# A state-space and MLP layer on one core: a third product with C on GpSimd, the fronts of images 2 and 3 raised in rank, and each norm's squares as one instruction

## The chip, the cores and the metric

The kernel runs on one core of a Trainium2 chip. The metric is the device time of the program in microseconds, as the median of its runs: 3404.53 us before the change (three runs, 3401.29 to 3411.84). The profiled execution has a span of 3393.6 us. The engines are named as the profile names them: PE is TensorE (matmuls), PEld its weight loads, DVE is VectorE, ACT is ScalarE, POOL is GpSimd, SP issues nearly all transfers.

## What is computed

The input is x of 8 images with 384 channels and 32 x 32 places (1024 tokens each), all in float32. One layer is applied:

```python
x = x + conv(_ln_c(x), ...)          # a selective state space, then an MLP
t = _to_tokens(x)
t = t + ffn(_ln_t(t), W1, b1, W2, b2)
```

The state-space part normalises each token, projects 384 channels to 2 x 768 (xm and z), runs a causal convolution of three taps and silu over xm (xc), projects xc to a step size dt, and to B and C of 16 states each, and then goes over the 1024 tokens of each image with

```python
hst = dA_t * hst + dBu_t                       # 768 x 16 states
y   = jnp.einsum('bdn,bn->bd', hst, C_t)       # sum over the 16 states
```

with dA = exp(dt A) and dBu = dt xc B. Then y + xc D is multiplied by silu(z), projected back to 384 channels (out_proj), and sent through an MLP 384 - 1536 - 384 with an exact gelu. The ffn that follows works with sign-binarised weights and quantises its activations over whole images by their largest absolute value. By its grouping of the batch it changes only images 0 to 4 (`NUM_GROUPS` is 5, one image each); images 5 to 7 get nothing from it.

## The kernel before, in words

**Stages.** For each image b there are four. The front `s1` (L523) loads x in two halves of 512 tokens, normalises (`norm`, L466), does the first projection (p_in) with the taps on DVE (L590), then xc, dbc, dt, dt x xc on POOL (L639), and the gate z (p_z). It hands dt, dt x xc, xc, z and the rows of B and C on through DRAM. The scan `s2` (L655, `scan` L668) does the recurrence. The back `s3` (L824) does out_proj (p_out) and the MLP (p_h, p_o). The `ffn` (L1022) follows for images 0 to 4 (p_y). Once, after the scan of image 0 is written down, `binarise` (L902) prepares the ffn's weights on PE, ACT and POOL.

**The scan.** It goes unit by unit, 12 in an image. A unit has four quads q of states, and each quad two tiles i = 0, 1: eight tiles of 128 x 1024. `scan_tile` (L782) takes for each tile these steps: exp on ACT writes da into PSUM (two buffers); POOL multiplies dtx with B into u (L798; u has nine buffers in SBUF); the recurrence runs on DVE (L802); then the product with C. That product is made on DVE (L819: the scan is written over da in PSUM, the product into u), or on POOL (L816: the scan is written over u, and POOL multiplies u in place). `on_pool` (L778) decides: before, tiles with i = 1 and odd q. Image 0 and image 7 are scanned in two halves of 512 tokens, and then a tile's two channel groups each have an own exp and scan of 512 columns, and the last state is kept (L810 on POOL, L813 on ACT). After each two quads (BATCH) TensorE sums the four tiles' states into py (`sums`, L719 to 732), which frees their u. At the end of a unit DVE adds xc D (L759) and POOL multiplies with z (L769).

**The order of the work.** The kernel first writes down all operations with a cost in microseconds, what they read and write and which buffers they take (`Plan.add`, L172). `Plan.run` (L216) then walks through a planned time and emits for each engine in turn the operation to do next, so that each engine has one fixed order, known before the run. `rank` (L250) sorts the operations that are ready: lane -1 (the sums) and lane 0 (the scan) first, then the fronts (lanes 1, 4, 11, 14) of images up to the one after that being scanned, then the rest, and fronts of later images last. On DVE and POOL operations that are not of the scan are preferred (L244). SLACK (L79) is a lag that the plan adds before the sums may start. Where TensorE would idle for over 0.7 us in the plan and an mm buffer is free, it emits fillers (`fill`, L375: a matmul of 256 columns on ones whose result nobody reads)[...].

**The norm.** `norm` sums over channels with three matmuls on ones (L473), subtracts the mean on DVE (L478), squares each of the three 128-channel blocks on ACT as an own instruction into one of two sq buffers, and after each square does four small matmuls on ones for the variance (L491 to 499). Then come sqrt on ACT, a reciprocal on DVE (L505), four matmuls that spread it (L512), and a multiplication on DVE (L517). The kernel has 26 norms.

```python
first = (1, b) if b <= scanned + 1 else (3, b)               # L259, the fronts
return POOL_TILES and i == 1 and q % 2 == 1                  # L780, on_pool
```

Of the kernel before, what the change touches and what calls it, by code (L numbers as in the profile page):

```python
# [26 lines left out]
F32 = mybir.dt.float32  # L27
AF = mybir.ActivationFunctionType
# [5 lines left out]
P = 128  # L34
B, C, L = 8, 384, 1024
KC = C // P
# [7 lines left out]
T = 512  # L44
# [8 lines left out]
TG = T // G  # L53
POOL_TILES = True
# [20 lines left out]
SIGNAL = 0.1  # L75
IDLE = 0.7
EARLY = 2
PATIENCE = 0.0
SLACK = 1.6  # L79
LOAD_TABLE = 1.29  # L80


def c_act(n):
    return 0.22 + n * 0.00084
# [10 lines left out]
class Clock:  # L95
# [4 lines left out]
    def __init__(self):  # L100
        self.window, self.busy, self.slow = 0, 0.0, True
# [38 lines left out]
class Fixed:  # L140


    ring = None
# [15 lines left out]
class Plan:  # L159
# [56 lines left out]
    def run(self):  # L216
# [6 lines left out]
        left, scanned = len(self.ops), 0  # L223
# [26 lines left out]
        def rank(op):  # L250


            lane, b = op.prio[:2]
            if lane <= 0:
                first = (lane, b)
            elif lane == 7:
                first = (EARLY, b)
            elif lane in (1, 4, 11, 14):
                first = (1, b) if b <= scanned + 1 else (3, b)  # L259
            else:  # L260
                first = (2, b)
            return (*first, op.prio[2])

        while left:
# [10 lines left out]
            if op.prio[0] == 0:  # L275
                scanned = max(scanned, op.prio[1])
            left -= 1
            if e == "PE":
                while now - free[e] > IDLE and self.spare.ring.free[0:] and (
# [3 lines left out]
                    ring = self.spare.ring  # L283
# [35 lines left out]
class Layer:  # L319
    def __init__(self, ctx, tc, a, out):  # L320
        self.tc, self.nc, self.a, self.out = tc, tc.nc, a, out
        self.plan = Plan()

        def pool(name, **kw):
            return ctx.enter_context(tc.tile_pool(name=name, bufs=1, **kw))

        self.const = pool("const")
        sbuf, psum, dram = pool("sbuf"), pool("psum", space=PSUM), pool("dram", space=DRAM)

        def ring(tag, bufs, where=sbuf):  # L330
            def make(shape, name):
                return where.tile(shape, F32, tag=tag, name=name, bufs=bufs)

            return Ring(make, bufs)

        self.rings = {

            "front": ring("front", 2), "t_f": ring("t_f", 2), "w_f": ring("w_f", 3),
            "dbc": ring("dbc", 1), "halo": ring("halo", 2),

            "dt_r": ring("dt_r", 3), "dtx_r": ring("dtx_r", 3), "u": ring("u", 9),
            "xr": ring("xr", 1), "zr": ring("zr", 1), "state": ring("state", 1),
            **{f"bc{i}": ring(f"bc{i}", 1) for i in range(2 * NQUAD)},
            "da": ring("da", 2, psum), "y": ring("y", 1, psum),

            "yg": ring("yg", 1), "hid": ring("hid", 2), "t_b": ring("t_b", 1), "w_b": ring("w_b", 3),
            "w6": ring("w6", 2), "w6_n": ring("w6_n", 2), "res": ring("res", 2),

            "t_n": ring("t_n", 2), "small": ring("small", 12),

            "mm": ring("mm", 3, psum), "sq": ring("sq", 2),
            "rstd": ring("rstd", 2),
        }

        def handed(name, shape):
            return Fixed(dram.tile(shape, F32, name=name))

        self.dram = {}
        for b in range(B):
            for name in ("dt", "dtx"):  # L360
                self.dram[name, b] = handed(f"{name}_d{b}", [DI, L])

            for name in ("xc", "z", "yg"):
                self.dram[name, b] = handed(f"{name}_d{b}", [NP, P, T])
            self.dram["rows", b] = handed(f"rows_d{b}", [2 * NS, L])
            if b < NQ:
                self.dram["mid", b] = handed(f"mid_d{b}", [C, L])
                self.dram["y1", b] = handed(f"y1_d{b}", [P, KH, L])
        self.bin = {
            "W1": handed("bin_w1", [KH, P, KC, P]), "W2": handed("bin_w2", [KC, P, KH, P]),  # L370
        }
        self.constants()

        self.plan.spare = self.piece("mm", [P, T], "spare")
        self.plan.fill = lambda: self.nc.tensor.matmul(  # L375
            self.plan.spare.real[:, : 2 * P], self.ones,
            self.ones.unsqueeze(1).to_broadcast([P, 2, P]), start=True, stop=True,
        )

    def piece(self, ring, shape, name):  # L380
# [3 lines left out]

    def constants(self):
        nc, a, const = self.nc, self.a, self.const
        self.ones = const.tile([P, P], F32, name="ones")
        nc.vector.memset(self.ones, 1.0)
        self.ident = ident = const.tile([P, P], F32, name="ident")
        make_identity(nc, ident)  # L390

        self.fold = const.tile([P, DQ], F32, name="fold")
        nc.vector.tensor_reduce(
            self.fold, ident.rearrange("p (d n) -> p d n", n=SQ), AX.X, ALU.add
        )
        self.edge = const.tile([P, KD, 2], F32, name="edge")
        self.eps_m = const.tile([P, 1], F32, name="eps_m")
        nc.vector.memset(self.eps_m, E1 * E2)
        self.eps_f = const.tile([P, 1], F32, name="eps_f")
        nc.vector.memset(self.eps_f, E_FFN)  # L400

        def vec(name, k):
            v = const.tile([P, k], F32, name=f"v_{name}")
            nc.scalar.dma_start(v, a[name])
            return v

        self.ln_w, self.ln_b, self.mlp_b2 = vec("ln_w", KC), vec("ln_b", KC), vec("mlp_b2", KC)
        self.conv_b, self.dt_b = vec("conv_b", KD), vec("dt_proj_b", KD)
        self.d_pair, self.d_unit = vec("D_pair", NP), vec("D", KD)
        self.mlp_b1 = vec("mlp_b1", KH)  # L410
        self.b1, self.b2 = vec("b1", KH), vec("b2", KC)
        self.conv_w = const.tile([P, KD, 3], F32, name="conv_w")
        nc.scalar.dma_start(self.conv_w, a["conv_w"])
        self.a_neg = const.tile([P, NJ * NQUAD], F32, name="a_neg")
        nc.scalar.dma_start(self.a_neg, a["A_log"])
        nc.scalar.activation(self.a_neg, self.a_neg, AF.Exp)
        nc.vector.tensor_scalar_mul(self.a_neg, self.a_neg, -1.0)
# [48 lines left out]
    def norm(self, t, eps, scale):  # L466

        nc, add = self.nc, self.plan.add
        p_sum = self.piece("mm", [P, T], "p_sum")

        def total():
            for k in range(KC):
                nc.tensor.matmul(  # L473
                    p_sum.real, self.ones, t.real[:, k, :], start=(k == 0), stop=(k == KC - 1)
                )

        add("PE", KC * MM, total, r=[t], w=[p_sum])
        add("DVE", c_dve(KC * T), lambda: nc.vector.scalar_tensor_tensor(  # L478
            t.real, p_sum.real.unsqueeze(1).to_broadcast([P, KC, T]), -1.0 / C, t.real,
            ALU.mult, ALU.add,  # L480
        ), r=[p_sum], w=[t])

        p_var = self.piece("mm", [P, TG], "p_var")
        for k in range(KC):
            sq = self.piece("sq", [P, T], "sq")
            self.act(
                lambda sq=sq: sq.real, lambda k=k: t.real[:, k, :], AF.Square, c_act(T),
                r=[t], w=[sq],
            )

            def var(k=k, sq=sq):  # L491
                for g in range(G):
                    nc.tensor.matmul(
                        p_var.real[g * DQ : (g + 1) * DQ, :], self.ones[:, :DQ],
                        sq.real[:, g * TG : (g + 1) * TG],
                        start=(k == 0), stop=(k == KC - 1),
                    )

            add("PE", 0.3, var, r=[sq], w=[p_var])
        rstd = self.piece("rstd", [P, TG], "rstd")  # L500
        self.act(
            lambda: rstd.real, lambda: p_var.real, AF.Sqrt, c_act(TG), r=[p_var], w=[rstd],
            table="sqrt", bias=eps, scale=scale,
        )
        add("DVE", 0.93, lambda: nc.vector.reciprocal(rstd.real, rstd.real), w=[rstd])  # L505
        p_r = self.piece("mm", [P, T], "p_r")

        def spread():
            for g in range(G):

                one = self.ident[:, g * DQ : g * DQ + 1].to_broadcast([P, P])
                nc.tensor.matmul(  # L512
                    p_r.real[:, g * TG : (g + 1) * TG], one, rstd.real, start=True, stop=True
                )

        add("PE", MM, spread, r=[rstd], w=[p_r])
        add("DVE", c_dve(KC * T), lambda: nc.vector.tensor_mul(  # L517
            t.real, t.real, p_r.real.unsqueeze(1).to_broadcast([P, KC, T])
        ), r=[p_r], w=[t])
# [257 lines left out]

    def on_pool(self, i, q):  # L778

        return POOL_TILES and i == 1 and q % 2 == 1  # L780

    def scan_tile(self, hcs, cols, n, dt_r, dtx_r, bq, cq, state, half, on_pool):  # L782
        nc, add = self.nc, self.plan.add
# [412 lines left out]
```

## Time and profile before

| | busy us | share of the span | instructions |
|---|---|---|---|
| PE | 3213.9 | 95% | 10356 |
| DVE | 2875.2 | 85% | 2179 |
| POOL | 2644.4 | 78% | 1312 |
| ACT | 2017.5 | 59% | 2278 |
| span | 3393.6 | | 32501 |

| operation | count | mean ns |
|---|---|---|
| u, product with B, POOL L798 | 768 | 2364 |
| scan of 1024 columns over da, DVE L802 | 432 | 2285 |
| scan of 1024 columns over u, DVE L802 | 144 | 2280 |
| product with C on DVE, L819 | 576 | 1221 |
| product with C on POOL, L816 | 192 | 2360 |
| exp of 1024 columns, ACT | 576 | 1116 |
| square of 512 columns, ACT | 78 | 624 and 621 |

The busy times are unions of an engine's instructions. A float32 matmul leaves two records on PE and two on PEld. Line L444 and line L460 are helpers (all large matmuls, all activations), so that groups are told apart by the names of their tiles. PEclk is the clock that the throttle granted TensorE, as a share of full speed; a matmul under a smaller clock is longer and counts as busy all the same. The scan starts on POOL at about 163 us and ends on DVE at about 3316 us; ahead of it lie fronts, behind it the back of image 7.

### The profile page before, as it was taken

The numbers are of one execution on the slowest core, as the hardware profiler recorded it, in microseconds if no ns is written. First come the engines' busy times: TensorE is split into PE (matmuls) and PEld (weight loads), VectorE is DVE, ScalarE is ACT, GpSimd is POOL, SyncE is SP. The second block draws the span as 40 slices with busy tenths as digits, with TensorE's granted clock in tenths as the row PEclk, the third lists the DMA queues.
The fourth block names the chain that finished last, engine by engine and source line by source line (L and its number), as shares of the span: only waits on it lengthen the run. The fifth ranks groups of instructions, "written<-read, shape, count | busy, mean of one in ns | idle before, by whom it ended". The sixth has DMA issues, their size and how long they took to land.

```text
span 3393.6 us, 32501 instructions
## 1 busy us (share of the span) xinstructions
PE 3213.9 (95%) x10356; PEld 1331.2 (39%) x10356; DVE 2875.2 (85%) x2179; ACT 2017.5 (59%) x2278; POOL 2644.4 (78%) x1312
## 2 busy tenths in 40 slices
PE   8987898999898999799999999999999999999999
PEld 3332333344333334343344444343333444443334
DVE  3677797899897999899989989899887999988990
ACT  4677557566754556645665656666657546565551
POOL 1787776788698878799868789776898788888870
PEclk9988998999999999899999999999999999999999
DMA  6887756766687556866579576975668656766542
GB/s 195 260 280 245 237 170 222 239 193 217 224 285 228 191 184 231 305 222 215 173 259 280 192 252 221 313 230 189 236 229 290 216 196 218 227 204 208 172 136 75
DMA packets 369370, 751.77 MB, mean 222 GB/s; under 512 B 35376, under 2 KB 112688, under 8 KB 369200
## 3 DMA queue, kind: packets, MB, share of 16 engines
q1 hardware_dynamic: 367472, 749.60, 67.8%
q8 instruction: 83, 1.36, 0.2%
q14 instruction: 87, 0.71, 0.1%
q10 hardware_dynamic: 1728, 0.09, 0.0%
HBM read 569.21 MB, written 180.36 MB: 221 GB/s over the span
## 4 chain that ended last, share of the span: by engine, by line
PE 63%; DVE 10%; DMA 9%; ACT 9%; POOL 4%; issue 3%; SPq 1%; ACTq 0%; DVEq 0%; POOLq 0%
PE p_y L444 16%; PE p_o L444 11%; PE p_h L444 10%; PE py L729 7%; DVE da L802 6%; PE p_out L444 6%; PE p_z L444 5%; PE p_in L444 4%; ACT da L460 3%; POOL u L798 2%; ACT L460 2%; DVE u L819 2%; DMA w_f<-in_in_proj_w 1%; PE spare L375 1%; PE p_dt L628 1%
## 5 line engine op out<-in xcount | busy, mean ns | idle before, releaser
L798 POOL TENSOR_TENSOR u<-dtx_r,bc 128x1024 f32<-128x1024 f32 x768 | 1796.0, 2364 | 376.6 <-PE py L729 324.6
L460 ACT ACTIVATE da<-dt_r,a_neg 128x1024 f32<-128x1024 f32 (+1 forms) x960 | 902.2, 945 | 705.3 <-DVE u L819 569.2
L802 DVE TENSOR_TENSOR_SCAN da<-da,u 128x1024 f32<-128x1024 f32 (+1 forms) x576 | 1163.9, 2021 | 183.8 <-ACT da L460 132.8
L819 DVE TENSOR_TENSOR u<-da,bc 128x1024 f32<-128x1024 f32 x576 | 703.1, 1221 | 18.4 <-ACT state L813 0.9
L816 POOL TENSOR_TENSOR u<-u,bc 128x1024 f32<-128x1024 f32 x192 | 453.0, 2360 | 117.9 <-DVE u L802 111.1
L444 PE MATMUL p_h<-t,w_b 128*128 128x512 f32 x1152 | 515.9, 600 | 18.2 <-DMA w_b<-in_mlp_w 9.4
L444 PE MATMUL p_o<-g,w 128*128 128x512 f32 x1152 | 511.0, 599 | 10.4 <-DMA w<-in_mlp_w 5.4
L802 DVE TENSOR_TENSOR_SCAN u<-da,u 128x1024 f32<-128x1024 f32 (+1 forms) x192 | 384.3, 2011 | 23.5 <-ACT da L460 20.0
L729 PE MATMUL py<-u,fold 128*32 128x512 f32 x3072 | 381.3, 611 | 5.4 <-POOL u L816 5.4
L444 PE MATMUL p_y<-gf,w_n 128*128 128x512 f32 x720 | 324.8, 606 | 26.4 <-ACT gf L460 21.8
L444 PEld LDWEIGHTS p_h<-t,w_b 128*128 128x128 f32 x1152 | 214.9, 191 | 309.5 <-issue 260.2
L444 PEld LDWEIGHTS p_o<-g,w 128*128 128x128 f32 x1152 | 216.5, 191 | 301.5 <-issue 285.1
L444 PE MATMUL p_y<-tn,w_b 128*128 128x512 f32 x720 | 327.6, 601 | 2.6 <-DVE tn L517 0.9
L460 ACT ACT_TABLE_LOAD x220 | 282.3, 1283 | 10.6 <-DVE xc L590 6.6
L444 PE MATMUL p_out<-yg,w 128*128 128x512 f32 x552 | 250.9, 607 | 9.9 <-ACT da L460 4.2
L444 PE MATMUL p_in<-t,w_f 128*128 128x512 f32 x504 | 232.2, 607 | 18.3 <-DMA w_f<-in_in_proj_w 12.1
L444 PE MATMUL p_z<-t,w_f 128*128 128x512 f32 x504 | 227.4, 597 | 6.2 <-DMA w_f<-in_in_proj_w 3.8
L444 PEld LDWEIGHTS p_y<-gf,w_n 128*128 128x128 f32 x720 | 136.7, 193 | 212.4 <-issue 180.8
L444 PEld LDWEIGHTS p_y<-tn,w_b 128*128 128x128 f32 x720 | 135.2, 192 | 180.5 <-issue 161.7
L802 DVE TENSOR_TENSOR_SCAN da<-da,state,u 128x512 f32<-128x512 f32 x144 | 184.9, 1284 | 22.9 <-ACT da L460 9.1
L590 DVE SCALAR_TENSOR_TENSOR xc<-p_in,conv_w,xc 128x511 f32<-128x511 f32 x192 | 141.1, 742 | 58.7 <-ACT halo L585 37.6
L729 PEld LDWEIGHTS py<-u,fold 128*32 128x32 f32 x3072 | 81.7, 110 | 273.4 <-issue 199.4
(100 smaller groups left out, 2758.3 us busy)
## 6 DMA issues: line engine op xcount, KB each, us to landing
dtx_r<-dtx_d SPq DMA_DIRECT2D x144, 512.0 KB, 5.4
dt_r<-dt_d SPq DMA_DIRECT2D x144, 512.0 KB, 5.3
w_b<-in_mlp_w SPq DMA_DIRECT2D x192, 192.0 KB, 2.6
w<-in_mlp_w SPq DMA_DIRECT2D x96, 384.0 KB, 3.5
w_f<-in_in_proj_w SPq DMA_DIRECT2D x168, 192.0 KB, 4.5
y_d<-y SPq DMA_DIRECT2D x120, 256.0 KB, 3.3
gf<-y_d SPq DMA_DIRECT2D x20, 1536.0 KB, 9.1
xc_d<-xc SPq DMA_DIRECT2D x32, 768.0 KB, 8.6
```

Of the source, the lines that this page charges most:

```text
L375: self.plan.fill = lambda: self.nc.tensor.matmul(self.plan.spare.real[:, : 2 * P], self.ones, self.ones.unsqueeze(1).to_broadcast([P, 2, P ...
L444: self.nc.tensor.matmul(p.real, w.real[:, w0 + k, :], t.real[:, k0 + k, :], start=start and k == 0, stop=stop and k == n - 1,)
L460: lambda: self.nc.scalar.activation(out(), in_(), func, **{k: v() if callable(v) else v for k, v in kw.items()}),
L590: nc.vector.scalar_tensor_tensor(xc.real[:, m, s:], pm.real[:, : T - s], tap[2 - s], xc.real[:, m, s:], ALU.mult, ALU.add,)
L628: add("PE", MM / 2, lambda i=i, k=k, pd=pd, dbc=dbc, w=w: nc.tensor.matmul(pd.real, w.real[i : i + R, k % KC, :], dbc.real[i : i + R, :], ...
L729: nc.tensor.matmul(py.real[p0 : p0 + DQ, :], self.fold, hc, start=(q == 0), stop=(q == NQUAD - 1),)
L798: add("POOL", 2.36, lambda: nc.gpsimd.tensor_mul(u.real, dtx_r.real, spread(bq)), r=[dtx_r, bq], w=[u])
L802: add("DVE", 0.13 + n * 0.0021, lambda k=k, col=col: nc.vector.tensor_tensor_scan(to.real[:, k, :], da.real[:, k, :], u.real[:, k, :], sta ...
L816: add("POOL", 2.36, lambda: nc.gpsimd.tensor_mul(u.real, u.real, spread(cq)), r=[cq], w=[u])
L819: add("DVE", 1.21, lambda: nc.vector.tensor_mul(u.real, da.real, spread(cq)), r=[da, cq], w=[u])
```

## The change

Four things are changed.

1. `on_pool` picks three of a unit's eight tiles, (i, q) = (0, 0), (0, 2) and (1, 0), in the place of (1, 1) and (1, 3). This moves products with C from DVE to POOL.
2. The fronts up to image 3 have the front's high rank from the start (FRONTS = 3), so that the fronts of images 2 and 3 come ahead of backs and ffn even while image 0 or 1 is scanned. SLACK goes from 1.6 to 1.4.
3. A norm's three squares are one ACT instruction over 128 x 1536, and its twelve variance matmuls are one piece in the plan. The ring sq has one buffer of three times the size.
4. To make room in SBUF, the ones are one column read as a broadcast, in the norm's matmuls and in the fillers, and the ring of small tiles has 7 buffers, not 12.

```diff
+FRONTS = 3
 PATIENCE = 0.0
-SLACK = 1.6
+SLACK = 1.4
...
             elif lane in (1, 4, 11, 14):
-                first = (1, b) if b <= scanned + 1 else (3, b)
+                first = (1, b) if b <= max(scanned + 1, FRONTS) else (3, b)
...
-            "t_n": ring("t_n", 2), "small": ring("small", 12),
+            "t_n": ring("t_n", 2), "small": ring("small", 7),
-            "mm": ring("mm", 3, psum), "sq": ring("sq", 2),
+            "mm": ring("mm", 3, psum), "sq": ring("sq", 1),
...
-            self.ones.unsqueeze(1).to_broadcast([P, 2, P]), start=True, stop=True,
+            self.one.to_broadcast([P, 2 * P]), start=True, stop=True,
...
-        self.ones = const.tile([P, P], F32, name="ones")
-        nc.vector.memset(self.ones, 1.0)
+        one = const.tile([P, 1], F32, name="one")
+        nc.vector.memset(one, 1.0)
+        self.one, self.ones = one, one.to_broadcast([P, P])
...
-        for k in range(KC):
-            sq = self.piece("sq", [P, T], "sq")
-            self.act(
-                lambda sq=sq: sq.real, lambda k=k: t.real[:, k, :], AF.Square, c_act(T),
-                r=[t], w=[sq],
-            )
-
-            def var(k=k, sq=sq):
+        sq = self.piece("sq", [P, KC, T], "sq")
+        self.act(lambda: sq.real, lambda: t.real, AF.Square, c_act(KC * T), r=[t], w=[sq])
+
+        def var():
+            for k in range(KC):
                 for g in range(G):
                     nc.tensor.matmul(
                         p_var.real[g * DQ : (g + 1) * DQ, :], self.ones[:, :DQ],
-                        sq.real[:, g * TG : (g + 1) * TG],
+                        sq.real[:, k, g * TG : (g + 1) * TG],
                         start=(k == 0), stop=(k == KC - 1),
                     )
 
-            add("PE", 0.3, var, r=[sq], w=[p_var])
+        add("PE", 0.9, var, r=[sq], w=[p_var])
...
     def on_pool(self, i, q):
 
-        return POOL_TILES and i == 1 and q % 2 == 1
+        return (i == 0 and q % 2 == 0) or (i == 1 and q == 0)
```

## The prediction

> **What bounds the kernel now.** I read the shares of busy time first, then the chain of waits, then the costliest groups, then the busy time of each engine image by image, and last the waits of POOL and ACT. The page:
>
> ```profile
> PE 3213.9 (95%) x10356; PEld 1331.2 (39%) x10356; DVE 2875.2 (85%) x2179; ACT 2017.5 (59%) x2278; POOL 2644.4 (78%) x1312
> ...
> PEclk9988998999999999899999999999999999999999
> ...
> PE 63%; DVE 10%; DMA 9%; ACT 9%; POOL 4%; issue 3%; SPq 1%; ACTq 0%; DVEq 0%; POOLq 0%
> ```
>
> TensorE is busy 95% of the span of 3393.6 us and carries 63% of the chain that ended last. Part of that is not work: the groups with shapes kept apart show the filler matmuls of L375 (their result is read by nobody), and the two products with C that the change exchanges, and the squares:
>
> ```profile
> L819 DVE TENSOR_TENSOR u<-da,bc 128x1024 f32<-128x1024 f32 x576 | 703.1, 1221 | 18.4 <-ACT state L813 0.9
> ...
> L816 POOL TENSOR_TENSOR u<-u,bc 128x1024 f32<-128x1024 f32 x192 | 453.0, 2360 | 117.9 <-DVE u L802 111.1 <-ACT xc L460 3.4 <-DMA yg_d<-xr 0.3
> ...
> L375 PE MATMUL spare<-ones 128*128 128x256 f32 x378 | 100.7, 408 | 1.3 <-DVE eps_f L400 1.1
> ...
> L460 ACT ACTIVATE sq<-t 128x512 f32<-128x512 f32 x48 | 28.8, 624 | 13.2 <-DVE t L478 13.0
> ```
>
> A float32 matmul leaves two records, so 378 records are 189 fillers of 100.7/189 = 0.533 us. TensorE's work without them is 3213.9 - 100.7 = 3113 us; the span has 180 us of idle and 101 us of fillers beyond it. Where these lie is seen in the stretches of single images (cut at the last L759 of each image; columns: length, then busy us and records of PE, PEld, DVE, ACT, POOL, then clock, DMA share, GB/s):
>
> ```profile
> 160.00:580.00 420.00, 365.35 (x1143) 149.57 (x1142) 329.51 (x298) 289.61 (x385) 317.41 (x185) 0.89 0.72 227
> 580.00:1000.00 420.00, 388.07 (x1301) 162.30 (x1300) 377.61 (x270) 257.91 (x271) 336.63 (x162) 0.94 0.69 227
> 1000.00:1380.00 380.00, 366.28 (x1186) 151.07 (x1185) 341.40 (x240) 210.77 (x222) 310.33 (x149) 0.98 0.67 220
> 1380.00:1760.00 380.00, 352.58 (x1181) 142.35 (x1180) 343.45 (x237) 223.03 (x218) 323.87 (x154) 0.96 0.69 229
> 1760.00:2120.00 360.00, 358.40 (x1151) 147.78 (x1149) 327.16 (x234) 223.16 (x233) 305.35 (x145) 1.00 0.75 241
> ...
> 2880.00:3316.00 436.00, 426.67 (x1333) 173.39 (x1331) 393.37 (x334) 247.24 (x339) 359.51 (x176) 1.00 0.59 189
> ```
>
> These are images 0, 1, 2, 3, 4 and 7. From image 4 on TensorE is busy 97 to 100% and its clock is whole: it is the bound there. In images 0 to 3 it idles 54.7 + 31.9 + 13.7 + 27.4 = 128 us, and the clock withholds 11%, 6%, 2% and 4% of the stretches, about 46 + 25 + 8 + 15 = 94 us, some 85 us of it under work. So about 213 us are lost in the first four images. VectorE is at 78 to 91% there, POOL at 76 to 85%. The waits:
>
> ```profile
> ACT da L460 <- DVE u L819: 569.2, 289, 6.8
> ...
> POOL u L798 <- PE py L729: 324.6, 94, 12.7
> ...
> POOL u L816 <- DVE u L802: 111.1, 48, 10.9
> ```
>
> POOL mostly waits for a u buffer, which comes free when TensorE has summed it: the scans are held by TensorE's queue more than TensorE by the scans (TensorE's own wait before py is 5.4 us in all).
>
> **What the Trainium skill says.** "GPSIMD Engine Reference", 3.1 Elementwise — side-by-side cycle accounting, measures a two-input float32 operation 1.96 times slower on GpSimd than on VectorE; the rows above have 2360 against 1221 ns, 1.93 times, so it agrees. The same page, 8. Key points, says that GpSimd's SBUF interfaces are shared with VectorE and contend with VectorE instructions with two SBUF inputs. Here da lies in PSUM, so scan and product take one operand from there; POOL's u took 2364 ns on average beside both, and the trace of before has no such contention to show. "TensorE: Matmul & The Clock Gate", What's actually happening: the clock is halved after an idle window of about 3.4 us and returns after a busy one; the trace agrees in kind (0.89 in the stretch with most idle time, 1.00 where there is next to none). "Perfetto Trace Analysis", Identifying the Most-Contended Engine, warns that matmul busy share does not tell the distance to the peak; that is why I take fillers and clock out before I call PE the bound.
>
> **The change part by part.**
>
> *Products.* Two of eight tiles per unit had their product on POOL, now three: 96 products of 768 move. VectorE loses 96 x 1.221 = 117 us (2875 to about 2758), POOL gains 96 x 2.360 = 227 us (2644 to about 2871). POOL then has the load that VectorE had, 85%. The scan's end lies behind about 2790 us of POOL work in 3150 us, 89%, as behind VectorE's before. The chain is not shorter in its longest engine, so I book nothing for it in the sum; the work that hides it is TensorE's. Gained beside it: a tile with its product on POOL gives its da back after the scan, 1.2 us sooner, and only ACT, 59% busy, waits for that. Lost: each product waits in POOL's queue for a scan, 117.9/192 = 0.61 us each until now, so 96 more bring 59 us of POOL idle. Behind the waiting product stand the next u of L798, and behind these the scans; POOL has 749 us of idle time, so my value is 0, the upper bound 59 us. The new pattern puts the products at the first tiles of a pair of quads and no longer at the last, so that VectorE's two tiles still run while POOL multiplies; this speaks for the lower end.
>
> *Early fronts and slack.* The rank of the fronts of images 2 and 3 is raised over backs and FFN while images 0 and 1 are scanned; the predicted lag of the sums goes from 1.6 to 1.4 us. The two programs' instruction orders show what comes of it together with the products: full-size matmuls ahead of the last sum of images 0, 1, 2, 3, 4 are 423, 738, 1092, 1446, 1818 instead of 414, 729, 1077, 1398, 1782, and fillers ahead of them 33, 51, 66, 89, 99 instead of 50, 89, 103, 106, 119; in all 160 instead of 189. Other TensorE work is equal. 29 fillers at 0.533 us are 15.4 us (nothing if all lay in true gaps; I count them whole, as TensorE has other work waiting in most of the span). Fillers mark the places where TensorE has nothing to do, and up to image 3 they fall by 17 of 106, 16%. I let the 213 us of idle and slow clock there fall by the same share: 34 us. The bounds are 0 (same gaps, merely elsewhere) and 40%, the fall up to image 1 (38/89 = 43%) and image 2 (37/103 = 36%), 85 us.
>
> *Squares.* 78 squares of 0.62 us (48.4 us) become 26 of 128x1536. The nearest row, ACT's y<-y,q of 128x1536, has 1564 ns: 40.7 us, so 8 us less on ACT, which waits 569 us for VectorE anyway: 0. The twelve variance matmuls of a norm now start after 1.56 us and not after 0.62 us, and they take 29.2/26 = 1.1 us: the norm ends up to 0.5 us later, at most 26 x 0.5 = 13 us, hidden where TensorE has other matmuls queued ahead, which is everywhere but in the first 30 us (2 norms, 1 us). One sq buffer makes the next norm wait for these 1.1 us: 0. The ones as a broadcast column, the smaller rings: the p_r matmuls load a broadcast already at 217 ns against about 207 for p_sum, 0.
>
> Sum: 3404.5 - 15.4 - 34 + 1 = 3356, rounded to 3355 us.
>
> **The rivals.**
>
> *POOL takes over as the bound.* For: 2871 us of work, 89% of the scanned stretch, and a two-input operation that no engine speeds up. Then images 1 to 6 go on at 360 to 420 us each, TensorE's removed fillers turn to idle time, and only a trifle of the 15 us remains: 3400 us. Against: POOL now waits 325 us for TensorE.
>
> *Waiting products, slower.* Half of the 59 us of waits falls on the chain from POOL over the scans to the sums, and the fillers still go: 3404.5 + 30 - 15 + 1 = 3420 us; with all of it 3449. For: L816 waits 111.1 us for scans, the longest 10.9. Against: the better place of the products.
>
> *The whole early loss shrinks.* With VectorE relieved and fronts at hand, images 0 to 2 lose 40% less: 3404.5 - 15 - 85 + 1 = 3305; with something of it given back in image 3, whose stretch gets 23 fillers where it had 3 (20 x 0.533 = 11 us), about 3316 us. For: no engine is full in image 0. Against: ACT and VectorE must do the earlier fronts in the same stretch, and both prefer them to scans.
>
> **How the numbers follow.** The forecast has 0.56, POOL as bound 0.16, slower by waits 0.15, the large gain 0.13. The range reaches from the large gain, 3316, to the slower case, 3420; I widen its foot a little, to 3312, for what of the 40% isn't given back. About 0.12 of chance lies outside at either end taken together, most of it above. Faster by over 0.3% (below 3394) is the forecast, the large gain and a small part of POOL as bound: 0.71. Within 0.3% is most of that rival: 0.14. Slower: 0.15.
>
> **What would show it.** Right: 320 filler records in the place of 378; PE idle plus missing clock in the first four images about 34 us less; VectorE near 2760 and POOL near 2870 us; POOL's wait for py still its largest. Wrong: PE idle growing from image 3 on while POOL stands above 95% (POOL as bound), L816 waiting far over 177 us (slower), a product or u on POOL longer than 2.4 us (contention that before did not show), or images 0 to 3 as long as before although fillers went.

## The result and the profile after

The changed kernel takes 3366.22 us (3356.93 to 3371.15) against 3408.19 us before; the ratio is 0.9874 with a 95% interval of 0.9842 to 0.9906. That is 42 us or 1.3% less, against 49 us forecast (3355 us), inside the range of 3312 to 3420 us. The two profiled executions lie nearer to each other, 3393.6 and 3369.4 us, so that the traces have 24 of the 42 us to show.

The page of the changed kernel, its busy times and the chain that ended last:

```profile
PE 3203.1 (95%) x10298; PEld 1327.3 (39%) x10298; DVE 2758.5 (82%) x2083; ACT 2005.1 (60%) x2212; POOL 2863.5 (85%) x1420
...
PE 67%; DMA 11%; DVE 7%; ACT 6%; POOL 4%; issue 3%; SPq 1%; DVEq 0%; POOLq 0%; ACTq 0%
```

The loads moved as worked out: VectorE lost 117 us, POOL gained 219, and POOL is now where VectorE was. In the chain VectorE went from 10 to 7%, while TensorE and transfers have more of it. The groups of the exchanged operations, shapes kept apart:

```profile
L815 POOL TENSOR_TENSOR u<-u,bc 128x1024 f32<-128x1024 f32 x288 | 678.8, 2364 | 162.5 <-DVE u L801 145.7 <-PE p_in L446 6.2 <-issue 4.0
...
L818 DVE TENSOR_TENSOR u<-da,bc 128x1024 f32<-128x1024 f32 x480 | 586.3, 1221 | 12.2
...
L376 PE MATMUL spare<-one 128*128 128x256 f32 x320 | 85.3, 406 | 1.9 <-ACT t L855 1.0 <-DVE eps_f L402 0.9
...
L462 ACT ACTIVATE sq<-t 128x1536 f32<-128x1536 f32 x16 | 23.6, 1475 | 10.3 <-DVE t L480 9.3 <-PE p_var L492 1.0
```

The two products did not become slower: 2364 and 1221 ns, against 2360 and 1221 before. The fillers are 160 for 85.3 us. What did change is POOL's waits (engine and line, what it waited for: us in all, times, longest):

```profile
POOL u L815 <- DVE u L801: 145.7, 56, 13.6
POOL u L797 <- DMA dtx_r<-dtx_d: 68.0, 21, 9.4
...
POOL u L797 <- PE py L728: 21.5, 7, 7.7
```

POOL had waited 324.6 us for TensorE to free a u; of that 21.5 us are left. VectorE waits for POOL's u in return: 160 us over both forms of the scan, where it had waited 55. First its waits before, then after:

```profile
DVE da L802 <- POOL u L798: 52.6, 21, 7.6
...
DVE u L802 <- POOL u L798: 2.6, 2, 1.6
```

```profile
DVE da L801 <- POOL u L797: 113.6, 30, 10.0
...
DVE u L801 <- POOL u L797: 46.4, 12, 9.6
```

By image: the prediction's stretches were cut too early, by 14 to 72 us. The last L759 of images 0 to 7 starts at 619, 1014, 1408, 1788, 2179, 2585, 2952 and 3316 us. Cut there, images 0 to 3 and 5 before (columns as in the prediction: length, busy us of PE, PEld, DVE, ACT, POOL, clock, DMA share, GB/s):

```profile
0.00:619.16 619.16, 538.65 (x1711) 226.71 (x1712) 441.48 (x404) 407.79 (x550) 416.92 (x247) 0.91 0.73 232
619.16:1013.78 394.62, 368.23 (x1213) 152.83 (x1212) 355.79 (x252) 238.26 (x244) 319.25 (x153) 0.95 0.68 227
1013.78:1407.83 394.05, 378.92 (x1250) 156.31 (x1250) 356.14 (x260) 223.12 (x239) 315.04 (x152) 0.98 0.68 220
1407.83:1788.04 380.21, 353.59 (x1169) 142.99 (x1170) 339.15 (x228) 223.42 (x218) 327.80 (x159) 0.96 0.68 229
...
2178.84:2584.75 405.91, 395.82 (x1313) 161.31 (x1308) 362.14 (x265) 255.67 (x264) 326.94 (x158) 1.00 0.71 235
```

And images 0 to 3 and 5 after the change, cut at its own last L758:

```profile
0.00:613.23 613.23, 533.30 (x1666) 222.76 (x1667) 424.29 (x397) 415.43 (x537) 448.54 (x270) 0.91 0.78 238
613.23:1002.14 388.91, 364.22 (x1246) 150.06 (x1245) 346.22 (x246) 241.31 (x246) 338.88 (x163) 0.95 0.71 227
1002.14:1393.85 391.71, 379.46 (x1257) 156.56 (x1256) 342.54 (x235) 228.44 (x233) 354.52 (x167) 0.98 0.73 235
1393.85:1792.27 398.42, 389.95 (x1280) 163.88 (x1279) 334.32 (x233) 237.15 (x235) 355.71 (x172) 0.98 0.72 231
...
2178.43:2541.78 363.35, 350.21 (x1138) 141.44 (x1137) 332.11 (x234) 220.66 (x220) 337.02 (x160) 0.98 0.72 230
```

Image 3 is 18 us longer and image 5 43 us shorter. That is TensorE work which changed places: in its order image 3 has 354 full matmuls and not 321, image 5 has 324 and not 372. The idle time of TensorE (length less PE's busy time) is 79.9, 24.7, 12.3 and 8.5 us in images 0 to 3, against 80.5, 26.4, 15.1 and 26.6 before. So early fronts filled next to nothing in images 0 to 2; the 18 us are in image 3. There a wait of 13.1 us of p_y for gf (the gelu of the ffn, queued on ACT behind a front's activations) is gone, which in the trace of before reads (start and length in us, what ran, in brackets the idle time before it):

```profile
1428.13 4.53 PE L444 MATMUL p_y<-gf,w_n 128*128 128x512 f32 x5 [13.12 <-ACT gf L460]
```

In images 4 to 7 idle time rose from 27 to 37 us, and the clock withheld 2% of image 5 and 1% of image 7, where before it stood at 1.00.

### The profile page after: what moved, and what is told of

Read it like the earlier page. It is cut to its first block, busy times and chain, and to the rows that moved or that the text cites. A ratio compares the mean times of both kernels' runs of the same rounds, so it can differ in the third digit from the quotient of the medians.

```text
span 3369.4 us, 32362 instructions
## 1 busy us (share of the span) xinstructions
PE 3203.1 (95%) x10298; PEld 1327.3 (39%) x10298; DVE 2758.5 (82%) x2083; ACT 2005.1 (60%) x2212; POOL 2863.5 (85%) x1420
## 4 chain that ended last, share of the span: by engine, by line
PE 67%; DMA 11%; DVE 7%; ACT 6%; POOL 4%; issue 3%; SPq 1%; DVEq 0%; POOLq 0%; ACTq 0%
PE p_y L446 15%; PE p_o L446 13%; PE p_h L446 11%; PE py L728 8%; PE p_out L446 5%; PE p_z L446 5%; PE p_in L446 4%; DVE da L801 4%; DMA w_f<-in_in_proj_w 3%; ACT da L462 2%; DMA w_b<-in_mlp_w 2%; ACT L462 1%; PE p_dt L627 1%; PE p_sum L475 1%; POOL u L797 1%
## 5 line engine op out<-in xcount | busy, mean ns | idle before, releaser
L797 POOL TENSOR_TENSOR u<-dtx_r,bc 128x1024 f32<-128x1024 f32 x768 | 1790.0, 2361 | 100.7 <-DMA dtx_r<-dtx_d 68.0
L801 DVE TENSOR_TENSOR_SCAN da<-da,u 128x1024 f32<-128x1024 f32 (+1 forms) x480 | 970.3, 2021 | 195.1 <-POOL u L797 111.3
L815 POOL TENSOR_TENSOR u<-u,bc 128x1024 f32<-128x1024 f32 x288 | 678.8, 2364 | 162.5 <-DVE u L801 145.7
L801 DVE TENSOR_TENSOR_SCAN u<-da,u 128x1024 f32<-128x1024 f32 (+1 forms) x288 | 572.6, 2010 | 68.1 <-ACT da L462 37.6
L818 DVE TENSOR_TENSOR u<-da,bc 128x1024 f32<-128x1024 f32 x480 | 586.3, 1221 | 12.2
L446 PE MATMUL p_h<-t,w_b 128*128 128x512 f32 x1152 | 517.6, 602 | 17.1 <-DMA w_b<-in_mlp_w 9.8
L728 PE MATMUL py<-u,fold 128*32 128x512 f32 x3072 | 388.9, 615 | 19.3 <-DVE u L818 9.9
L446 PEld LDWEIGHTS p_y<-tn,w_b 128*128 128x128 f32 x720 | 135.6, 192 | 181.5 <-issue 162.5
L462 ACT ACTIVATE g<-p_h,v_mlp_b 128x512 f32<-128x512 f32 x192 | 128.0, 679 | 118.2 <-PE p_h L446 118.0
```

Of the source, the lines that this page charges most:

```text
L446: self.nc.tensor.matmul(p.real, w.real[:, w0 + k, :], t.real[:, k0 + k, :], start=start and k == 0, stop=stop and k == n - 1,)
L462: lambda: self.nc.scalar.activation(out(), in_(), func, **{k: v() if callable(v) else v for k, v in kw.items()}),
L728: nc.tensor.matmul(py.real[p0 : p0 + DQ, :], self.fold, hc, start=(q == 0), stop=(q == NQUAD - 1),)
L797: add("POOL", 2.36, lambda: nc.gpsimd.tensor_mul(u.real, dtx_r.real, spread(bq)), r=[dtx_r, bq], w=[u])
L801: add("DVE", 0.13 + n * 0.0021, lambda k=k, col=col: nc.vector.tensor_tensor_scan(to.real[:, k, :], da.real[:, k, :], u.real[:, k, :], sta ...
L815: add("POOL", 2.36, lambda: nc.gpsimd.tensor_mul(u.real, u.real, spread(cq)), r=[cq], w=[u])
```

## The experiments

One sum is used for all of them: the span is TensorE's work (its busy time without fillers), the fillers and its idle time. Where there are fillers, their records lie over those of other matmuls for about 10 us in all, and the column of work is that much too low. And two places are read: where the scan ends (start of the last L758 or its like), and how many of the 2919 full matmuls TensorE's order leaves behind the last sum of the scans. The kernel before was timed anew beside each set of experiments, with medians from 3398 to 3412 us, so kernels of different sets are compared by their ratio to it. The ends of the scan before, after, and after with the old products:

```profile
3316.21 0.75 DVE L759 SCALAR_TENSOR_TENSOR xr<-xr,v_D,py 128x512 f32<-128x512 f32 x1 [5.48 <-PE py L729]
...
3282.44 0.75 DVE L758 SCALAR_TENSOR_TENSOR xr<-xr,v_D,py 128x512 f32<-128x512 f32 x1 [5.15 <-PE py L728]
...
3336.41 0.75 DVE L758 SCALAR_TENSOR_TENSOR xr<-xr,v_D,py 128x512 f32<-128x512 f32 x1 [5.48 <-PE py L728]
```

| kernel | ratio to before (interval) | work us | fillers us | idle us | scan ends | matmuls left |
|---|---|---|---|---|---|---|
| before | 1 | 3113 | 100.7 | 180 | 3316 | 85 |
| changed | 0.9874 (0.9842 to 0.9906) | 3118 | 85.3 | 166 | 3282 | 96 |
| changed, FRONTS = 0 | 1.0170 (1.0135 to 1.0205) | 3125 | 129.7 | 211 | 3263 | 231 |
| changed, old products | 1.0009 (0.9996 to 1.0022) | 3134 | 79.0 | 201 | 3336 | 85 |
| changed, SLACK = 1.6 | 1.0013 (0.9995 to 1.0032) | 3138 | 75.7 | 205 | 3305 | 126 |
| changed, old squares | 0.9991 (0.9980 to 1.0003) | 3138 | 76.5 | 189 | 3275 | 144 |
| before + products | 0.9963 (0.9944 to 0.9982) | 3106 | 113.8 | 173 | 3256 | 153 |
| before + fronts | 0.9939 (0.9924 to 0.9954) | 3124 | 96.9 | 166 | 3289 | 108 |
| changed, LOAD_TABLE 1.28 | 0.9910 (0.9883 to 0.9937) | 3115 | 93.7 | 173 | 3269 | 126 |
| changed, no fillers | 0.9892 (0.9854 to 0.9931) | 3149 | 0 | 215 | 3278 | 96 |
| changed, p_h lighter | 0.9831 (0.9781 to 0.9881) | 2999 | 85.1 | 262 | 3269 | 84 of 2727 |
| changed, VectorE lighter | 0.9846 (0.9805 to 0.9888) | 3103 | 83.1 | 163 | 3262 | 96 |
| changed, POOL lighter | 0.9826 (0.9775 to 0.9876) | 3109 | 84.9 | 151 | 3258 | 96 |
| changed, p_h and POOL lighter | 0.9727 (0.9705 to 0.9749) | 2991 | 84.6 | 242 | 3241 | 84 of 2727 |

**One part undone at a time.** Theory 1 is that of the prediction.

```diff
-FRONTS = 3
+FRONTS = 0
```

> The changed kernel with FRONTS = 0, so that the fronts of images 2 and 3 get their high rank only when the scan comes near them; products, slack and squares stay changed. TensorE's order then has 254 fillers in the place of 160. Theory 1 (TensorE's queue is the bound, its empty places are the measure, the fronts fill them): 94 more fillers at 0.533 us bring about 50 us, 3416 us, the time before or worse. Rival (VectorE's relief by the moved products makes the gain): the time stays within 10 us of 3366. Rival 2 (the gain is the squares or the slack): also near 3366.

It took 3468.20 us: slower than the kernel before by 1.7%, and 3% above the changed one, twice what theory 1 said. The scan ends 20 us sooner than in the changed kernel, but 231 matmuls remain, and they take 203 us. The direction is theory 1's, the size is not.

```diff
-        return (i == 0 and q % 2 == 0) or (i == 1 and q == 0)
+        return POOL_TILES and i == 1 and q % 2 == 1
```

> The changed kernel with two of eight products on POOL at the old places; fronts, slack and squares stay changed. TensorE's order has 151 fillers, 9 fewer than the changed kernel. Theory 1 (TensorE's queue is the bound): the time stays at 3366 or falls by up to 5 us, 3360. Rival (the move of products makes the gain): the time goes back to about 3400. VectorE should stand near 2875 us, POOL near 2640 us.

It took 3411.56 us. This is the rival's number, although the order has fewer fillers than the changed kernel; theory 1 falls here. The waits of POOL are those of before:

```profile
POOL u L797 <- PE py L728: 321.5, 90, 18.6
```

```diff
-SLACK = 1.4
+SLACK = 1.6
```

> The changed kernel with the slack of 1.6 us in the plan; the rest stays changed. TensorE's order has 143 fillers, 17 fewer. Theory 1: 9 us less than the changed kernel, 3357. Rival (the shorter slack gives u back sooner and makes part of the gain): 5 to 20 us more, 3371 to 3386.

It took 3416.46 us, where theory 1 had 3357, and more than the rival allowed, too. SLACK is read by the plan alone: but for 17 fillers this kernel makes the same operations, in another order. The next kernel keeps all but the squares, the single sq buffer, the ones as a column and the smaller ring of small tiles:

```diff
-        sq = self.piece("sq", [P, KC, T], "sq")
-        self.act(lambda: sq.real, lambda: t.real, AF.Square, c_act(KC * T), r=[t], w=[sq])
...
+        for k in range(KC):
+            sq = self.piece("sq", [P, T], "sq")
+            self.act(
+                lambda sq=sq: sq.real, lambda k=k: t.real[:, k, :], AF.Square, c_act(T),
+                r=[t], w=[sq],
+            )
```

> The kernel before with the products, fronts and slack of the changed one, but three squares by norm, two sq buffers and the ones as a full tile. TensorE's order has 144 fillers, 16 fewer than the changed kernel. Theory 1: the squares are worth nothing by themselves, the time is 3357 to 3366. Rival (one square in the place of three saves ACT's time and TensorE's waits): 5 to 15 us more, 3371 to 3381.

It took 3403.50 us. So each of three parts takes the whole gain with it when undone, and the fourth takes more. The parts do not add. And fillers do not count the loss: these three orders have 143 to 151 of them against 160, and are 37 to 50 us slower.

**The load of an engine, in an unchanged order.** If TensorE, VectorE or POOL were the bound, work taken from it alone would come back in the time. Three kernels do that:

```diff
             for k in range(n):
+                if light and k == 1:
+                    continue
...
-        self.matmuls(p, w, t, 0, KC, True, True, r, claim)
+        self.matmuls(p, w, t, 0, KC, True, True, r, claim, light=name == "p_h")
```

> The changed kernel in unchanged order on every engine, with one of the three matmuls of each p_h left out (192 of 576; the MLP's first product then lacks a third of its channels), 192 x 0.86 = 165 us less on TensorE. Theory 1 (TensorE is the bound): the time falls by 90 to 165 us, to 3200 to 3275. Rival (POOL, at 85%, or VectorE is the bound): it falls by 0 to 20 us.

```diff
-            add("DVE", 1.21, lambda: nc.vector.tensor_mul(u.real, da.real, spread(cq)),
-                r=[da, cq], w=[u])
+            add("DVE", 1.21, lambda: nc.vector.tensor_mul(
+                u.real[..., : n // 2], da.real[..., : n // 2], spread(cq)[..., : n // 2]
+            ), r=[da, cq], w=[u])
```

> The changed kernel in unchanged order, with VectorE's products with C made for the first half of the columns only (the rest of u then holds what POOL wrote), 480 x about 0.53 = 255 us less on VectorE. Theory 1 (TensorE is the bound): the time falls by 0 to 15 us. Rival (VectorE is the bound): by 100 us or more.

```diff
-            add("POOL", 2.36, lambda: nc.gpsimd.tensor_mul(u.real, u.real, spread(cq)),
-                r=[cq], w=[u])
+            add("POOL", 2.36, lambda: nc.gpsimd.tensor_mul(
+                u.real[..., : n // 2], u.real[..., : n // 2], spread(cq)[..., : n // 2]
+            ), r=[cq], w=[u])
```

> The changed kernel in unchanged order, with POOL's products with C made for the first half of the columns only (the rest of u keeps the scan's state), 288 x about 1.09 = 314 us less on POOL. Theory 1 (TensorE is the bound): the time falls by 0 to 15 us. Rival (POOL has become the bound): by 80 us or more, since DVE's 160 us of waits for POOL's u go.

They took 3342.86, 3347.96 and 3340.98 us. By their spans (3346.2, 3349.4 and 3344.4 against 3369.4) 165 us less on TensorE (192 x 0.859 us) gave 23, 240 less on VectorE (2758.5 to 2518.3) gave 20, and 306 less on POOL gave 25; by their ratios to before it is 15, 10 and 16 us, not clear of noise, as their intervals overlap that of the changed kernel. For VectorE and POOL theory 1 had expected 0 to 15 us, and about that came; it is the first of the three that speaks against it. None of the three edits brought back more than a small part of the work that it took out. Where TensorE's 165 us went can be read from the page of the kernel with lighter p_h:

```profile
PE 3084.5 (92%) x9914; PEld 1262.6 (38%) x9914; DVE 2758.2 (82%) x2083; ACT 2002.3 (60%) x2212; POOL 2862.7 (86%) x1420
```

TensorE's busy time fell by 118.6 us only, as its mean clock fell from 0.969 to 0.956 (43 us more withheld over the span) and the rest of its matmuls took 46 us longer; and its idle time rose from 166 to 262 us, 96 more. 46 + 96 + 23 = 165. Most of the new idle time stands before p_h itself, 94.8 us against 17.1:

```profile
PE p_h L448 <- DMA w_b<-in_mlp_w: 40.2, 21, 6.3
PE p_h L448 <- ACT g L464: 38.7, 16, 5.4
```

In the changed kernel these waits are 9.8 and 7.0 us. A shorter p_h thus runs into the transfers of its own weights and into the gelu that follows it on ACT. What less work elsewhere on TensorE would bring was not run. Two engines lightened together, with both edits above:

> The changed kernel in unchanged order with both TensorE and POOL lightened: 192 of 576 p_h matmuls left out (165 us) and POOL's products with C made for half the columns (306 us). Theory 2 (TensorE and POOL are two bounds of almost equal length, so that taking away one gave only 23 and 25 us): the time falls by 70 us or more, below 3300. Rival (no engine's load but the waits between the engines' fixed orders set the time): it falls by 25 to 50 us, about the sum of the two at most, 3316 to 3341.

The time was 3316.46 us, the span 51.5 us below the changed kernel, where the two gave 23 and 25. The number stands at the edge of the rival's expectation and far from the 70 us of two bounds that hide each other. By the spans the savings about add. By the ratios it is 50 us against 15 and 16, more than the sum; the interval of each of the two is 17 us wide to either side and allows both readings. What fits all four runs is that each engine's work is on the chain for a small part, and that most of what it does not do becomes waiting for others.

**The fillers.** The edit takes out the allocation and the call of the filler and leaves the plan's clock as it was:

```diff
-                    self.spare.real = ring.make(self.spare.shape, self.spare.name)
-                    self.fill()
```

> The changed kernel in unchanged order without the 160 fillers. If each filler costs its 0.533 us, as the prediction's working took it: 85 us less, 3281 us. If the fillers lie in gaps of TensorE: 0 to 15 us less, with as much more idle time. If they hold the clock up: the granted clock falls below 0.96 and the time is over 3366.

It took 3363.59 us, its ratio is 0.9892 against 0.9874: no difference that the intervals show. Its page has:

```profile
PE 3149.4 (94%) x9978; PEld 1269.4 (38%) x9978; DVE 2760.5 (82%) x2083; ACT 2004.1 (60%) x2212; POOL 2865.1 (85%) x1420
```

Of 85.3 us of fillers, 10 had lain over the records of other matmuls, 48 became idle time (166 to 215), 21 went into slower work (3128, which is 3118 with those 10 added, to 3149; the clock of 0.963 against 0.969 withholds 19 us more), and 5 came off the span. So a filler is worth about what it costs, and counting 0.533 us for each was wrong.

**One part alone, and an order of the same work.** Theory 2, made from the results so far, has the time as the scan's end plus what is left of TensorE's work. The first kernel makes the edit of the products alone in the kernel before, the second the edits of the fronts alone.

> The kernel before with the new choice of products alone (three of eight on POOL). TensorE's order then has 227 fillers and leaves 153 of 2919 full matmuls behind the last sum, where the kernel before leaves 85. Theory 2 (the moved products shorten the scans, but the time is the scan's end plus the TensorE work left behind it): the scan ends at 3270 to 3295 us in the place of 3316, and 153 x 0.86 = 132 us follow: 3405 to 3430, no gain. Rival A (the move is worth its gain by itself): 3365 to 3380. Rival B (the move does nothing to the scan): the scan ends near 3316 and the time is 3440 or more.

> The kernel before with FRONTS = 3 alone. TensorE's order has 189 fillers, as before, and leaves 108 full matmuls behind the last sum. Theory 2 (fronts move TensorE's work ahead, but without the moved products the scans are no faster): the scan ends near 3316 and 93 us follow, 3400 to 3420. Rival A (early fronts are the gain by themselves): 3365 to 3385.

With the products alone the time was 3395.75 us, 0.4% below before: the scan ends 60 us sooner (3256.3, ahead of all that was expected), and 153 matmuls, 136 us, follow it. The order has put 68 fewer full matmuls ahead of the last sum, 68 x 0.859 = 58 us: scans were exchanged for TensorE work, almost one to one. Rival A falls, and so does B; the time is 9 us below theory 2's. POOL's wait for py is 32.6 us. With the fronts alone it was 3388.95 us, 0.6% below, between theory 2 and rival A: the scan does end sooner, at 3289, which theory 2 had not, and 97 us follow. The last kernel keeps the whole change and alters a cost in the plan that has no part in it:

```diff
-LOAD_TABLE = 1.29
+LOAD_TABLE = 1.28
```

> The changed kernel with all its parts, and one cost in the plan that the change does not touch altered by 0.01 us (LOAD_TABLE 1.28 in the place of 1.29). The work is equal; only the order differs: 178 fillers, 126 full matmuls behind the last sum in the place of 96. Theory 3 (the gain belongs to this one order, and neighbouring orders of the same plan differ by as much as the gain): the time is 3380 to 3410. Rival (the gain is that of the change's parts, whatever the order in detail): 3356 to 3376.

It took 3381.08 us, 1 us inside theory 3's range and 5 us outside the rival's; its ratio is 0.9910. The same work in a neighbouring order is about 12 us slower than the changed kernel, though the intervals overlap, and about 31 us faster than before. This neighbour keeps about 70% of the gain. But SLACK and FRONTS, too, are read by the plan alone, so that the kernels with SLACK = 1.6 and with FRONTS = 0 are further orders of the same work, fillers apart, and they stand at 1.0013 and 1.0170. The four orders lie 3% apart, more than the gain. How much of the gain belongs to the changed work, and how much to this one order, is not settled.

## Why the prediction was right, and where its steps were not

The time is right, by 11 us, and by luck: the sum's two main terms do not hold.

- **TensorE as the bound.** The page's 95%, the chain's 63% and POOL's wait for py led to it. It did not stand the one test that was made: 165 us taken from p_h gave 23. But 78 of them became waits before p_h, most of them for its own weights and its gelu, and no other product was lightened, so the test weakens this reading more than it settles it. TensorE is one of three engines that run in fixed orders with loads close to one another.
- **Products, booked at nothing.** This is the step that failed. The loads were right (2758 and 2871 forecast, 2758.5 and 2863.5 measured), and the conclusion "the chain is not shorter in its longest engine, so I book nothing" was not. Alone the products bring 0.4%, and undone in the changed kernel they cost 1.4%. The profile had a sign of it: POOL waited 325 us for u buffers, so its 2644 us were no limit to be kept away from, and 219 us more were done in that time. In the six kernels with the new choice and otherwise whole work this wait of the first product for py is 8 to 33 us; in the three with the old one it is 290 to 325. The prediction named this wait as speaking against POOL as the bound, and did not draw the other conclusion, that it is room for POOL work. Its sign for this, "POOL's wait for py still its largest", was wrong.
- **Fillers, 15.4 us.** They fell by exactly 15.4 us (100.7 to 85.3), and this is worth nothing that could be measured, since all 85 us together are worth 5.
- **34 us of idle time and slow clock in images 0 to 3.** With the right cuts the idle time there fell from 148.6 to 125.3 us and the withheld clock from about 96 to about 89: 30 us, close to the number. But image 3 has 25 of them, 18 of idle time with its one gf wait and 7 of clock, and images 0 to 2, from which it was argued, gave 5 us of idle time and nothing of clock. Not foreseen were the 10 us of idle time and 12 us of slow clock that images 4 to 7 gave back. And the fall of the fillers as a measure of the loss is refuted by the three orders with fewer fillers and more time. That both numbers agreed is chance.
- **Squares, 0 us.** The durations are as estimated or less (1475 and 1479 ns against 1564), ACT lost 8 us of squares, and the later end of the norm shows: TensorE's wait before p_r went from 12.2 to 21.6 us, 9 more of the 13 allowed. Undone they cost 1.2%, but in another order, with 144 matmuls left behind the scan and not 96; this part's own worth was not measured alone.
- **The rivals.** POOL as the bound fell (306 us less gave 25). The waiting products cost 162.5 us of POOL's idle time, 45 more than before and not 59, and the time did not rise. The large gain fell with images 0 to 2, which kept their idle time.

What stands in the place of the forecast's reason: the moved products take work off VectorE and put it into waits of POOL, and the scans end sooner, by 60 us in the kernel before and by 54 in the changed one. That VectorE's relief is what lets them is argued, not shown: 240 us less on it in a fixed order moved the scan's end by 20 us only, and the edit changed the number and the places of POOL's products together. Where the order answers by leaving TensorE work for the end, as with the products alone (58 us) and most of all without fronts (231 matmuls), little or nothing is gained. In the changed kernel, with new against old products, the scan ends 54 us sooner, 96 matmuls and not 85 follow it (11 x 0.859 = 9 us), and the span is 44 us shorter: 35 us less idle time of TensorE, 16 us less work time at a higher clock (0.969 against 0.967), 6 us more fillers. Fronts, slack and squares change what is left, and where TensorE waits. So much the runs show. Why just this combination has 166 us of idle time where the three with one part undone have 189 to 205 isn't settled. Nor is it whether the gain is more than a lucky order: few orders of equal work were timed. The squares and the slack alone weren't run, nor three products on POOL at other places.

## What to carry to other kernels

An engine's idle time that waits for a buffer to come back can be room for more work on that engine, as the 325 us of POOL were for 219 us here; look at these waits before calling a move worth nothing. In a kernel whose engines run in fixed orders close to one another, test a bound by lightening one engine in the same order, and see in the trace whether the freed time becomes a wait of the lightened operation itself: if little comes back, judge a change by where the stage ends and what work is left behind it, not by a sum of busy times. Settings of a planner are to be measured together, and next to several orders of equal work: here such orders differed by more than the gain.

## What the runs showed of the hardware that was not expected

Less work on TensorE made the rest of its work slower. The records of full matmuls that follow each other without a gap start 429 ns apart in the trace of before where the whole clock is granted, and 853 ns where half of it is. With 165 us of matmuls less the mean clock went from 0.969 to 0.956 and the others took 46 us longer; without the fillers it went to 0.963 and they took 21 us longer. This is what the Trainium skill, "TensorE: Matmul & The Clock Gate", What's actually happening, says in kind of a clock that follows recent activity; its size here, about a quarter of the work removed, had not been in the working.
